# Weighing hyperedge blocks from PSUM in a fixed VectorE order, and spacing out the inverse degrees

## The chip, the cores and the metric

The kernel runs on one core of one Trainium2 chip. A core has TensorE (PE in the profile; PEld is its weight load), VectorE (DVE), ScalarE (ACT), GpSimd (POOL) and SyncE (SP, which only issues transfers here). Each works through its own list of instructions in order; a framework places the semaphores between them. SBUF is the working memory, PSUM the small memory that TensorE writes its products into, HBM the main memory. The metric is the device time of one execution in microseconds, the median of several.

## What is computed

Four graph layers on x (8 batches, 2048 nodes, 64 features) share one adjacency matrix. The change touches the first, whose core is cut from the reference here:

```python
h = x @ W
alpha = softmax(where(H.T > 0, leaky_relu(h @ a_node), NEG))         # nodes of a hyperedge
agg = einsum('ben,bnf->bef', alpha, h)                                # hyperedge features
beta = sigmoid((h @ a_gn)[:, None, :] + (agg @ a_ge)[:, :, None])
all_he = elu(beta[..., None] * h[:, None] + (1 - beta[..., None]) * agg[:, :, None])
coefs1 = softmax(where(H > 0, attn_scores(elu(agg))[:, None, :], NEG))
g = einsum('bne,benf->bnf', coefs1, all_he)                           # what the change computes
deg = maximum(adj.sum(-1), 1.0)[:, None]
industry = einsum('nm,bmf->bnf', adj / deg, x @ W_ind)                # uses the inverse degrees
```

The next layer uses 1 / sqrt(1 + row sum of the adjacency), which is taken from the same degrees.

## The kernel before

Most (node, hyperedge) pairs are empty. The kernel sorts the nodes by how many hyperedges they belong to and cuts them into 16 tiles of 128 nodes, one node a partition. Tile t has as many slots as its richest node needs: 12 for tile 0, then 5, 5, 4, 4, 4, four times 3, five times 2, and 1; 57 in all. One slot of one tile is a **block**: 128 nodes times 512 values (8 batches of 64 features). A loop over tiles and slots runs through the blocks:

- Three matmuls build z in a PSUM tile `pz`: the node's own row in two pieces (`hrh`, `hrl`, a high and a low part) through an identity, and the hyperedge's row through a one-hot matrix `o`.
- VectorE scales z in place by the ratio `R` (L793). ScalarE takes y = exp(z - 1) (L795). VectorE forms the elu from both, y = min(max(z, 1), y), into SBUF (L797); it is one above the elu, which is taken off later.
- VectorE weighs it with the softmax coefficient `co`: in the tile's first block into the sum `acc` (L800), otherwise in place in y (L802), and GpSimd adds y to acc (L803). After a tile's last block GpSimd scatters acc to HBM, `gs_hbm` (L805).

The PSUM tag "mm" has three buffers. They hold pz, and in between the transposed slot numbers of a coming tile (`slots`, once a tile), the transposed degrees `pdc` and four rows of inverse degrees `pinv`. A pz is free again when its last reader, L797, is done. The tag "y" has three SBUF buffers, acc two.

`begin(t)`, called in the first block of the tile ahead, fetches rows by an indirect transfer on GpSimd (L275), splits a row into its two pieces (ScalarE L167, GpSimd L168), issues small matmuls into `ps` and has VectorE compute R and co (L761, L764, L765, L767).

Between the blocks' matmuls the loop puts **filler**: `fill(n)` takes n steps of a generator, `products`, each step one 128x512 matmul of x times the adjacency, for use later in the layer. A block has five filler steps, and three more in the first block of a tile. `products` computes pair 0's first half, then the degrees of both halves of the columns (`degrees`, 64 matmuls with ones, its result evacuated in turns by ScalarE and VectorE at L110), then pair 0's second half and the other pairs. In pair 0's second half, from the third row tile on, every filler matmul also advances the generator `inverses` by one pass. It transposes the degrees, adds one (L366), lets GpSimd raise that to the power -0.5 (L367, `dinv`), overwrites the same SBUF tile with the degree of at least 1 (L368) and its reciprocal (L369), waits 20 passes, and then every four passes spreads a quarter of the reciprocals over a row, which ScalarE copies out (L378) and SP stores in `inv_hbm` (L379). The tile of these copies has two buffers.

TensorE's instructions are pinned to the order in which the program issues them (`keep_in_program_order`), as are GpSimd's row fetches and adjacency loads (two of the latter a block while there are any). The other engines' order in this loop is chosen by the framework's scheduler when the program is built. After the loop comes a stage that mixes the results; its TensorE list starts with 24 and 28 more filler steps before it needs what the scatters wrote.

Of the kernel before, what the change touches and what calls it, by code (L numbers as in the profile page):

```python
# [30 lines left out]
F32 = mybir.dt.float32  # L31
# [5 lines left out]
AF = mybir.ActivationFunctionType  # L37
ALU = mybir.AluOpType
AX = mybir.AxisListType
# [17 lines left out]
def tile_gnn_fast(  # L57
# [24 lines left out]
    nc = tc.nc  # L82
# [3 lines left out]
    P = 128  # L86
# [255 lines left out]
    def products():  # L342

        deg1 = hy.tile([P, NT], F32, name="deg1")

        def degrees(g):
            du = pph.tile([P, 2, C], F32, tag="ph", name=f"du{g}", bufs=2)
            for t in range(NT):
                for i in range(2):
                    mm(  # L350
                        du[:, i, :], lhsT=ones_r, rhs=adj_c(t, 2 * g + i), start=t == 0, stop=t == NT - 1
                    )
                    yield
            for i in range(2):
                c = 2 * g + i
                r = slice(c * P // NCH, (c + 1) * P // NCH)
                evacuate(deg4[r, :], du[r, i, :])

        def inverses():

            pdc = places["small"]([P, JT, P], "pdc")
            for j in range(JT):
                transpose(pdc[:, j, :], deg4[:, cols(j, P)])
            pdc = pdc.rearrange("p j (c r) -> p c j r", c=NCH)[:, :, :, 0]
            d1 = deg1.rearrange("p (c j) -> p c j", c=NCH)
            nc.vector.tensor_scalar(d1, pdc, 1.0, None, op0=ALU.add)  # L366
            nc.gpsimd.tensor_tensor(dinv, deg1, neg_half[:, :NT], ALU.pow)  # L367
            nc.vector.tensor_scalar(d1, pdc, 1.0, None, op0=ALU.max)  # L368
            nc.vector.reciprocal(deg1, deg1)  # L369
            for _ in range(20):  # L370
                yield
            for c in range(NCH):
                pt = places["small"]([P, C], "pinv")
                for j in range(JT):
                    k = c * JT + j
                    transpose(pt[:, cols(j, P)], deg1[:, k:k + 1].to_broadcast([P, P]))
                row = va.tile([P, C], F32, tag="ut", name="inv", bufs=2)
                nc.scalar.copy(row, pt)  # L378
                nc.sync.dma_start(inv_hbm[:, cols(c)], row)  # L379
                for _ in range(4):  # L380
                    yield

        for p in range(NP):
            for g in range(2):
                own = (2 * g, 2 * g + 1)
                ug = pph.tile([P, 2, C], F32, tag="ph", name="ug", bufs=2)
                u = {c: ug[:, c % 2, :] for c in own}
                turning = inverses() if p == 0 and g == 1 else iter(())
                for t in range(NT):
                    for i in range(2):  # L390
                        for c in own:
                            mm(
                                u[c], lhsT=part[t // JT][i][:, t % JT, :], rhs=adj_c(t, c),
                                start=t == 0 and i == 0, stop=t == NT - 1 and i == 1,
                            )
# [346 lines left out]
    with ExitStack() as pb_scope:  # L742
        pps = pb_scope.enter_context(tc.tile_pool(name="pb_ps", bufs=1, space=PSUM))
        places["small"] = lambda shape, name: pps.tile(shape, F32, tag="mm", name=name, bufs=3)
        pl = pb_scope.enter_context(tc.tile_pool(name="pl", bufs=1))

        def begin(t):
# [12 lines left out]
            R = pl.tile([P, 13, B], F32, tag="R", name="R", bufs=2)  # L760
            nc.vector.tensor_tensor(  # L761
                R[:, 0:S], ps[:, 0:S, 0, :], hrow[:, None, BF:BF + 8].to_broadcast([P, S, B]), ALU.add
            )
            nc.vector.tensor_reduce(R[:, S], ps[:, 0:S, 1, :].rearrange("p s b -> p b s"), AX.X, ALU.add)  # L764
            nc.vector.reciprocal(R[:, 0:S + 1], R[:, 0:S + 1])  # L765
            co = pl.tile([P, 12, B], F32, tag="co", name="co", bufs=2)
            nc.vector.tensor_tensor(  # L767
                co[:, 0:S], ps[:, 0:S, 1, :], R[:, S:S + 1, :].to_broadcast([P, S, B]), ALU.mult
            )
            return S, both, ohs, R, co  # L770


        tiles = [*range(NT - 2), NT - 1, NT - 2]
        now = begin(0)
        slots(tiles[1], pps, "mm", 3)
        for k, t in enumerate(tiles):
            S, both, ohs, R, co = now
            acc = pl.tile([P, B, F], F32, tag="acc", name="acc", bufs=2)
            for s in range(S):
                pz = pps.tile([P, C], F32, tag="mm", name="pz", bufs=3)  # L780
                for i, (l, r) in enumerate(((ident_r, both[0]), (ident_r, both[1]), (ohs[s], tab2))):
                    mm(pz, lhsT=l, rhs=r, start=i == 0, stop=i == 2)
                if s == 0 and k + 1 < NT:
                    fill(3)
                    now = begin(tiles[k + 1])
                fill(5)
                for _ in range(2):
                    if to_load:
                        load_adj(*to_load.pop(0))
# [3 lines left out]
                nc.vector.tensor_tensor(z, z, R[:, s, :, None].to_broadcast([P, B, F]), ALU.mult)  # L793
                y = pl.tile([P, B, F], F32, tag="y", name="y", bufs=3)
                nc.scalar.activation(y, z, AF.Exp, bias=-1.0)  # L795

                nc.vector.scalar_tensor_tensor(y, z, 1.0, y, op0=ALU.max, op1=ALU.min)  # L797
                cb = co[:, s, :, None].to_broadcast([P, B, F])
                if s == 0:
                    nc.vector.tensor_tensor(acc, y, cb, ALU.mult)  # L800
                else:
                    nc.vector.tensor_tensor(y, y, cb, ALU.mult)  # L802
                    nc.gpsimd.tensor_tensor(acc, acc, y, ALU.add)  # L803

            nc.gpsimd.indirect_dma_start(  # L805
                out=gs_hbm[:], out_offset=bass.IndirectOffsetOnAxis(ap=order[:, t:t + 1], axis=0),
                in_=acc.rearrange("p b f -> p (b f)"), in_offset=None,
            )

    hrp_scope.close()  # L810
    hy_scope.close()
# [1793 lines left out]
```

## Time and profile before

| what | us |
|---|---|
| median of three runs (1749.34 to 1750.75) | 1750.03 |
| the profiled execution's own time | 1747.23 |
| its span | 1745.0 |
| TensorE busy over the span | 1662.8 (95%) |
| VectorE, ScalarE, GpSimd busy | 832.9, 588.9, 573.6 |
| first and last matmul of the blocks (pz) start | 67.0 and 223.7 |
| last scatter issued | 231.7 |

The block loop takes about 165 us of the 1745. Lines of the profile name the engine, the source line, the operation and its tiles (out<-in); "x57" is the count, then come busy time and the mean of one in ns, then the engine's idle time just before them and what ended it. L172 is the helper through which most matmuls go, L175 that of the transposes, so these are told apart by tile names. Tile names are shortened by the profile (`co1` and `co2` are one name). Matmul durations overlap: a 128x512 matmul shows 0.39 to 0.40 us, but a filled queue starts one every 0.23.

### The profile page before, as it was taken

The page shows a single profiled execution, that of the slowest core. Times are in us where ns is not written, and L with a number is a line of the kernel's source. Part 1 is how long each engine was busy: PE and PEld are TensorE (multiplying, and loading weights), DVE is VectorE, ACT ScalarE, POOL GpSimd, SP SyncE. Part 2 cuts the span into 40 slices and gives each one's busy share as a digit, 9 for nine tenths or more (in the row PEclk, how much of TensorE's full clock was granted, in tenths as well). Part 3 has the DMA queues.
Part 4 walks back from the last instruction along what each step waited for, and adds up shares of the span by engine and source line. Part 5 has one row for each costly group of instructions (what it writes and reads, how often), then busy time and mean ns, then how long its engine had stood idle before and what let it go on. Part 6 is the DMA issues. An engine that isn't in the chain of part 4 may idle for free. (4 is left out here: it accounts for less than half of the span.)

```text
span 1745.0 us, 27987 instructions
## 1 busy us (share of the span) xinstructions
PE 1662.8 (95%) x11196; PEld 1214.8 (70%) x11196; DVE 832.9 (48%) x1547; ACT 588.9 (34%) x1031; POOL 573.6 (33%) x515
## 2 busy tenths in 40 slices
PE   6888899999989999999999989999989999999996
PEld 4666666666664444468788878888768877878775
DVE  7679945678642221210137147777623433433332
ACT  1345533434321212112213257878512222222221
POOL 4578845556534443422023001222310200202001
PEclk9899999999999999999999989999989999999998
DMA  9743344444340000017344547585571121211111
GB/s 334 253 158 124 103 131 140 151 140 145 97 141 6 30 19 12 24 66 292 111 140 130 137 105 157 133 171 131 150 273 43 49 61 43 61 47 42 57 43 39
DMA packets 171180, 195.83 MB, mean 112 GB/s; under 512 B 71536, under 2 KB 116336, under 8 KB 169760
## 3 DMA queue, kind: packets, MB, share of 16 engines
q1 hardware_dynamic: 160096, 154.54, 30.0%
q0 software_dynamic: 8544, 30.68, 5.3%
q10 hardware_dynamic: 2400, 8.72, 1.4%
q8 instruction: 90, 1.47, 0.4%
q14 instruction: 50, 0.41, 0.1%
HBM read 126.72 MB, written 67.17 MB: 111 GB/s over the span
## 5 line engine op out<-in xcount | busy, mean ns | idle before, releaser
L172 PE MATMUL ua<-pt,xn 128*128 128x512 f32 x512 | 230.2, 592 | 1.4 <-DVE pt L1150 1.4
L172 PEld LDWEIGHTS ua<-pt,xn 128*128 128x128 f32 x512 | 96.9, 190 | 111.1 <-issue 104.0
L1502 DVE COPY w_half<-pw 128x512 f32<-128x512 f32 x160 | 109.7, 705 | 91.2 <-PE pw L172 90.6
L1498 ACT COPY w_half<-pw 128x1024 f32<-128x1024 f32 x128 | 129.8, 1014 | 51.4 <-PE pw L172 51.4
L172 PE MATMUL py<-w_half,xg 128*32 128x128 f32 x4096 | 142.6, 280 | 1.2 <-issue 1.2
L172 PE MATMUL u<-adj,v0h 128*128 128x512 f32 x384 | 134.0, 426 | 1.1 <-ACT h L1800 1.1
L172 PE MATMUL u<-adj_more,v2h 128*128 128x512 f32 x384 | 126.5, 408 | 0.0
L172 PEld LDWEIGHTS py<-w_half,xg 128*32 128x32 f32 x4096 | 111.6, 138 | 18.9 <-issue 2.1
L172 PE MATMUL u<-adj,v0l 128*128 128x512 f32 x384 | 124.6, 402 | 0.0
L172 PE MATMUL u<-adj_more,v2l 128*128 128x512 f32 x384 | 124.2, 400 | 0.0
L172 PE MATMUL pw<-est,wst 64*128 64x256 f32 x1024 | 111.2, 322 | 4.9 <-ACT w_half L1498 2.7
L1156 POOL TENSOR_TENSOR acc<-acc,pt 128x512 f32<-128x512 f32 x60 | 76.5, 1274 | 104.3 <-DVE pt L1150 103.6
L172 PEld LDWEIGHTS pw<-est,wst 64*128 64x128 f32 x1024 | 84.5, 189 | 27.6 <-ACT w_half L1498 20.0
L1150 DVE TENSOR_SCALAR pt<-pt 128x512 f32<-128x512 f32 x64 | 29.6, 462 | 153.0 <-ACT pt L1149 152.8
L1709 ACT CAST ar<-fcav 128x512 fp32r<-128x512 f32 x64 | 39.5, 618 | 166.8 <-DMA fcav<-in_adj_t 165.9
L172 PE MATMUL u<-adj_more,v3l 128*128 128x512 f32 x288 | 94.2, 403 | 0.0
L172 PE MATMUL u<-adj,v1h 128*128 128x512 f32 x288 | 93.7, 403 | 0.0
L1149 ACT ACTIVATE pt<-s 128x512 f32<-128x512 f32 x64 | 38.0, 598 | 164.8 <-PE s L172 164.8
L172 PE MATMUL u<-adj_more,v3h 128*128 128x512 f32 x288 | 93.6, 403 | 0.0
L1710 DVE SCALAR_TENSOR_TENSOR ar<-fcav,ar 128x512 f32<-128x512 f32 x64 | 44.7, 698 | 100.9 <-ACT ar L1709 100.9
L172 PE MATMUL u<-adj,v1l 128*128 128x512 f32 x288 | 92.0, 397 | 0.0
L1681 POOL TENSOR_TENSOR x<-x,rows 128x512 f32<-128x512 f32 x16 | 22.7, 1439 | 210.8 <-PE pt L175 129.3
(406 smaller groups left out, 3282.6 us busy)
## 6 DMA issues: line engine op xcount, KB each, us to landing
fcav<-in_adj_t SPq DMA_DIRECT2D x64, 256.0 KB, 2.9
u_hbm<-ut SPq DMA_DIRECT2D x48, 256.0 KB, 2.8
xg<-u_hbm SPq DMA_DIRECT2D x24, 512.0 KB, 8.5
adj<-in_adj_t POOLq DMA_DIRECT2D x16, 512.0 KB, 7.7
adj_more<-in_adj_t POOLq DMA_DIRECT2D x16, 512.0 KB, 7.7
adj_hbm<-adj_more SPq DMA_DIRECT2D x16, 512.0 KB, 5.5
x_hbm<-r SPq DMA_DIRECT2D x28, 256.0 KB, 2.7
hs_hbm<-st ACTq DMA_DIRECT2D x8, 584.0 KB
```

Of the source, the lines that this page charges most:

```text
L172: tc.keep_in_program_order(nc.tensor.matmul(*args, **kw))
L1149: nc.scalar.activation(pt, s, AF.Exp)
L1150: nc.vector.tensor_scalar(pt, pt, 1.0, None, op0=ALU.max)
L1156: nc.gpsimd.tensor_tensor(accs[c], accs[c], pt, ALU.add)
L1498: pin(nc.scalar.copy(dst, pw.rearrange("p j o n -> p n (j o)")))
L1502: pin(copy(dst[:, :, 2 * j:2 * j + 2], bank.rearrange("p o n -> p n o")))
L1681: nc.gpsimd.tensor_tensor(xs, xs, b2.to_broadcast([P, JT, P]), ALU.add)
L1709: nc.scalar.copy(ar, seen_a)
L1710: nc.vector.scalar_tensor_tensor(ar.bitcast(F32), seen_a, 1.0, ar.bitcast(F32), op0=ALU.mult, op1=ALU.not_equal, accum_out=left[:, t, k:k ...
```

## The change

The elu is written back into PSUM, over z, and weighed from there; in a block that isn't a tile's first the product goes to a new SBUF tile y, which shares the tag "y" and its three buffers with the exp's result. The weighing of a block is put off: it is held in a list `rest` and issued in the next block, between that block's exp and its elu. With it go the GpSimd add and, behind a tile's last block, the scatter. R and co of the next tile are computed by `ratios()`, which is issued after the elu of the tile's first block and no longer in `begin`. All VectorE instructions of the loop are held in program order. In `inverses`, the degree of at least 1 and its reciprocal come 16 passes after the power has been issued, the first row 4 passes later, and the rows 11 passes apart. The degrees' evacuations are given to ScalarE and VectorE by name, VectorE's held in order.

```diff
@@ degrees
-                evacuate(deg4[r, :], du[r, i, :])
+                if i:
+                    tc.keep_in_program_order(nc.vector.tensor_copy(deg4[r, :], du[r, i, :]))
+                else:
+                    nc.scalar.copy(deg4[r, :], du[r, i, :])
@@ inverses
-            nc.vector.tensor_scalar(d1, pdc, 1.0, None, op0=ALU.add)
+            kept = tc.keep_in_program_order
+            kept(nc.vector.tensor_scalar(d1, pdc, 1.0, None, op0=ALU.add))
             nc.gpsimd.tensor_tensor(dinv, deg1, neg_half[:, :NT], ALU.pow)
-            nc.vector.tensor_scalar(d1, pdc, 1.0, None, op0=ALU.max)
-            nc.vector.reciprocal(deg1, deg1)
-            for _ in range(20):
+            for _ in range(16):
+                yield
+            kept(nc.vector.tensor_scalar(d1, pdc, 1.0, None, op0=ALU.max))
+            kept(nc.vector.reciprocal(deg1, deg1))
+            for _ in range(4):
                 yield
...
-                for _ in range(4):
+                for _ in range(11):
                     yield
@@ begin: the four VectorE instructions move into a function, each held
+            def ratios():
+                hold(nc.vector.tensor_tensor(
+                    R[:, 0:S], ps[:, 0:S, 0, :], hrow[:, None, BF:BF + 8].to_broadcast([P, S, B]), ALU.add
+                ))
...
+            return S, both, ohs, R, co, ratios
@@ the loop
         now = begin(0)
+        now[-1]()
         slots(tiles[1], pps, "mm", 3)
+        rest = []
+
+        def weighed(acc, z, cb, first, t):
+            if first:
+                hold(nc.vector.tensor_tensor(acc, z, cb, ALU.mult))
+            else:
+                y = pl.tile([P, B, F], F32, tag="y", name="y", bufs=3)
+                hold(nc.vector.tensor_tensor(y, z, cb, ALU.mult))
+                nc.gpsimd.tensor_tensor(acc, acc, y, ALU.add)
+            if t is not None:
+                nc.gpsimd.indirect_dma_start(
+                    out=gs_hbm[:], out_offset=bass.IndirectOffsetOnAxis(ap=order[:, t:t + 1], axis=0),
+                    in_=acc.rearrange("p b f -> p (b f)"), in_offset=None,
+                )
...
-                nc.vector.tensor_tensor(z, z, R[:, s, :, None].to_broadcast([P, B, F]), ALU.mult)
-                y = pl.tile([P, B, F], F32, tag="y", name="y", bufs=3)
-                nc.scalar.activation(y, z, AF.Exp, bias=-1.0)
-
-                nc.vector.scalar_tensor_tensor(y, z, 1.0, y, op0=ALU.max, op1=ALU.min)
+                hold(nc.vector.tensor_tensor(z, z, R[:, s, :, None].to_broadcast([P, B, F]), ALU.mult))
+                e = pl.tile([P, B, F], F32, tag="y", name="e", bufs=3)
+                nc.scalar.activation(e, z, AF.Exp, bias=-1.0)
+                if rest:
+                    rest.pop()()
+
+                hold(nc.vector.scalar_tensor_tensor(z, z, 1.0, e, op0=ALU.max, op1=ALU.min))
+                if s == 0 and k + 1 < NT:
+                    now[-1]()
                 cb = co[:, s, :, None].to_broadcast([P, B, F])
-                if s == 0:
-                    nc.vector.tensor_tensor(acc, y, cb, ALU.mult)
-                else:
-                    nc.vector.tensor_tensor(y, y, cb, ALU.mult)
-                    nc.gpsimd.tensor_tensor(acc, acc, y, ALU.add)
-
-            nc.gpsimd.indirect_dma_start(
-                out=gs_hbm[:], out_offset=bass.IndirectOffsetOnAxis(ap=order[:, t:t + 1], axis=0),
-                in_=acc.rearrange("p b f -> p (b f)"), in_offset=None,
-            )
+                rest.append(lambda z=z, acc=acc, cb=cb, s=s, t=t, S=S: weighed(
+                    acc, z, cb, s == 0, t if s == S - 1 else None
+                ))
+        rest.pop()()
```

More of the change, by code (lines that the diff above doesn't have):

```diff
@@ L745, in tile_gnn_fast @@
         pl = pb_scope.enter_context(tc.tile_pool(name="pl", bufs=1))
+        hold = tc.keep_in_program_order
         def begin(t):
@@ L760, in begin @@
             R = pl.tile([P, 13, B], F32, tag="R", name="R", bufs=2)
-            nc.vector.tensor_tensor(
-                R[:, 0:S], ps[:, 0:S, 0, :], hrow[:, None, BF:BF + 8].to_broadcast([P, S, B]), ALU.add
-            )
-            nc.vector.tensor_reduce(R[:, S], ps[:, 0:S, 1, :].rearrange("p s b -> p b s"), AX.X, ALU.add)
-            nc.vector.reciprocal(R[:, 0:S + 1], R[:, 0:S + 1])
-            co = pl.tile([P, 12, B], F32, tag="co", name="co", bufs=2)
[L767 to L770, printed above, removed]
+            co = pl.tile([P, 12, B], F32, tag="co", name="co", bufs=2)
+            def ratios():
+                hold(nc.vector.tensor_tensor(
+                    R[:, 0:S], ps[:, 0:S, 0, :], hrow[:, None, BF:BF + 8].to_broadcast([P, S, B]), ALU.add
+                ))
+                hold(nc.vector.tensor_reduce(
+                    R[:, S], ps[:, 0:S, 1, :].rearrange("p s b -> p b s"), AX.X, ALU.add
+                ))
+                hold(nc.vector.reciprocal(R[:, 0:S + 1], R[:, 0:S + 1]))
+                hold(nc.vector.tensor_tensor(
+                    co[:, 0:S], ps[:, 0:S, 1, :], R[:, S:S + 1, :].to_broadcast([P, S, B]), ALU.mult
+                ))
+            return S, both, ohs, R, co, ratios
         tiles = [*range(NT - 2), NT - 1, NT - 2]
         now = begin(0)
+        now[-1]()
         slots(tiles[1], pps, "mm", 3)
+        rest = []
[11 more added lines that the diff above has]
+                )
         for k, t in enumerate(tiles):
-            S, both, ohs, R, co = now
+            S, both, ohs, R, co, _ = now
             acc = pl.tile([P, B, F], F32, tag="acc", name="acc", bufs=2)
@@ L792, in tile_gnn_fast @@
                 z = pz.rearrange("p (b f) -> p b f", f=F)
-                nc.vector.tensor_tensor(z, z, R[:, s, :, None].to_broadcast([P, B, F]), ALU.mult)
-                y = pl.tile([P, B, F], F32, tag="y", name="y", bufs=3)
-                nc.scalar.activation(y, z, AF.Exp, bias=-1.0)
-                nc.vector.scalar_tensor_tensor(y, z, 1.0, y, op0=ALU.max, op1=ALU.min)
-                cb = co[:, s, :, None].to_broadcast([P, B, F])
-                if s == 0:
-                    nc.vector.tensor_tensor(acc, y, cb, ALU.mult)
-                else:
-                    nc.vector.tensor_tensor(y, y, cb, ALU.mult)
-                    nc.gpsimd.tensor_tensor(acc, acc, y, ALU.add)
-            nc.gpsimd.indirect_dma_start(
-                out=gs_hbm[:], out_offset=bass.IndirectOffsetOnAxis(ap=order[:, t:t + 1], axis=0),
-                in_=acc.rearrange("p b f -> p (b f)"), in_offset=None,
-            )
+                hold(nc.vector.tensor_tensor(z, z, R[:, s, :, None].to_broadcast([P, B, F]), ALU.mult))
[6 more added lines that the diff above has]
+                    now[-1]()
+                cb = co[:, s, :, None].to_broadcast([P, B, F])
+                rest.append(lambda z=z, acc=acc, cb=cb, s=s, t=t, S=S: weighed(
+                    acc, z, cb, s == 0, t if s == S - 1 else None
+                ))
+        rest.pop()()
     hrp_scope.close()
```

## The prediction

> **What bounds the kernel now.** I read the page's slices first, then busy time by stretch for the stage that the diff touches, then its groups with shapes kept apart, then the waits, then the timeline of single engines. The page's chain of waits reaches back only to 1286 us, so it says nothing of this stage; the stretches must. The scatters of the 16 tiles (108.4, 119.4, 136.7, 146.7, 160.4, 169.3, 176.4, 184.3, 193.0, 202.6 ... 224.3, 227.8, 231.7) give the time of each tile. Busy time by stretch, 68 to 238 us:
> ```profile
> core 0: us, PE busy (x) PEld busy (x) DVE busy (x) ACT busy (x) POOL busy (x), PEclk, DMA share, GB/s
> 68.00:102.00 34.00, 30.22 (x114) 22.59 (x113) 24.77 (x39) 13.13 (x37) 23.73 (x28) 0.88 1.08 368
> 102.00:120.00 18.00, 16.22 (x72) 12.57 (x72) 17.48 (x31) 10.19 (x29) 14.06 (x11) 1.00 0.16 55
> 120.00:156.00 36.00, 28.20 (x133) 21.44 (x131) 27.86 (x49) 17.86 (x42) 29.33 (x22) 1.00 0.36 113
> 156.00:190.00 34.00, 32.19 (x145) 25.61 (x146) 33.51 (x60) 21.39 (x60) 29.39 (x23) 1.00 0.31 106
> 190.00:224.20 34.20, 29.15 (x117) 21.02 (x116) 29.39 (x57) 17.86 (x44) 29.98 (x25) 0.95 0.35 111
> 224.20:238.30 14.10, 14.08 (x59) 10.69 (x57) 4.14 (x8) 2.89 (x5) 4.93 (x5) 1.00 0.16 60
> ```
> TensorE runs one in-order list of matmuls, blocks and filler alike, and after the last block it is full (14.08 of 14.10). Up to 500 us it stays near full, so what the change can win is TensorE's idle time in these blocks: 3.8, 1.8, 7.8, 1.8 and 5.1 us, 20.2 in all. VectorE is behind it in the second and fourth stretch, GpSimd close to it in the last. The groups of the blocks (67 to 232 us):
> ```profile
> L803 POOL TENSOR_TENSOR acc<-acc,y 128x512 f32<-128x512 f32 x41 | 56.9, 1388 | 14.5 <-DVE y L802 11.9 <-DVE R L764 1.3 <-PE pz L172 0.4
> L802 DVE TENSOR_TENSOR y<-y,co 128x512 f32<-128x512 f32 x41 | 40.4, 1002 | 0.2
> L793 DVE TENSOR_TENSOR pz<-pz,R 128x512 f32<-128x512 f32 x57 | 38.3, 686 | 9.6 <-PE pz L172 7.2 <-ACT o L300 1.3 <-issue 1.0
> L797 DVE SCALAR_TENSOR_TENSOR y<-pz,y 128x512 f32<-128x512 f32 x57 | 37.8, 677 | 7.2 <-ACT y L795 6.6
> L800 DVE TENSOR_TENSOR acc<-y,co 128x512 f32<-128x512 f32 x16 | 17.4, 1086 | 0.9 <-DMA gs_hbm<-acc,order 0.9
> ```
> The two weighings (L802, L800) are the only ones of these that read both inputs from SBUF, and the only ones far above 0.69 us. Spread of three operations (min/median/max):
> ```profile
> L802 DVE TENSOR_TENSOR y<-y,co x41: 674/691/3445, 78.1 to 227.7; 128x512 f32<-128x512 f32 x41
> L800 DVE TENSOR_TENSOR acc<-y,co x16: 675/866/2372, 71.7 to 227.1; 128x512 f32<-128x512 f32 x16
> L885 DVE TENSOR_TENSOR ind<-pi,inv x16: 673/690/693, 240.1 to 442.3; 128x512 f32<-128x512 f32 x16
> ```
> L885 is the new weighing's shape exactly (PSUM and SBUF in, SBUF out) and never goes over 0.693. VectorE's timeline at the inverse degrees:
> ```profile
> 125.43 0.69 DVE L797 SCALAR_TENSOR_TENSOR y<-pz,y 128x512 f32<-128x512 f32 x1
> 130.84 0.17 DVE L368 TENSOR_SCALAR deg<-pdc 128x16 f32<-128x16 f32 x1 [4.72 <-POOL dinv L367]
> 130.93 0.68 DVE L802 TENSOR_TENSOR y<-y,co 128x512 f32<-128x512 f32 x1
> ```
> L368 overwrites what GpSimd's power still reads, and all of VectorE's blocks stand behind it. TensorE's and VectorE's own waits:
> ```profile
> PE pz L172 <- DVE y L797: 10.3, 13, 1.7
> PEld pz L172 <- issue: 10.5, 9, 2.0
> DVE pz L793 <- PE pz L172: 7.2, 10, 1.6
> DVE y L797 <- ACT y L795: 6.6, 7, 2.4
> ```
> The first is the third PSUM buffer coming free at L797.
>
> [...] L802 reaches 3.445 us, L793 with one SBUF input never passes 0.700. [...] the trace shows no such difference (0.690 against 0.691), so I charge none.
>
> **The change part by part.**
>
> *Weighing from PSUM.* 57 weighings at 0.69 are 39.3 us instead of 40.4 + 17.4 = 57.8: 18.5 us of VectorE gone. GpSimd's adds go from 1.388 to about 1.29 (their median): 41 x 0.1 = 4 us. L797 now writes PSUM; L793, which does so, takes 0.686 against 0.677: +0.5 us[...]. The exp's tile and the weighed tile are now two allocations of the same three buffers, so exp of block s+3 still waits for the add of block s, as before: nothing, provided that GpSimd isn't later.
>
> *Order and lateness.* VectorE's order is scale(s), weigh(s-1), elu(s). In a filled queue such operations start 0.60 apart. The elu waits for scale 0.69 + exp 0.60 + about 0.09 of handover (75.09 to 76.45 in the timeline is 1.36), while the weighing fills 0.6 of that: a block is 1.36 + 0.60 = 1.96, rounded to 1.98, if ScalarE is free. Queued behind a late exp now stand the elu, the next scale and the next weighing; GpSimd and the PSUM buffers wait for those. ScalarE is 50% busy, 48 us of it in 164 with other pieces of 0.3 to 0.6: 0.29 x 0.3 = 0.1 us on average, up to 0.6 where one full piece is ahead each time; I take 0.2, so 2.18 a block. Ratios of the next tile (R and co) cost 0.55 to 0.75 a tile as before, now after elu(0), where the tile still has a block or more to go: nothing, or 0.7 late in tiles of one or two blocks.
>
> *PSUM held longer.* A block's buffer comes free at weigh(s), inside block s+1, instead of at the elu: some 1.3 us later. The third buffer covers this except where the slot transpose takes it, once a tile: then the next three matmuls (0.95 from the waiting one to the scale, at 95.30 to 96.27) stand against one elu of 0.6, so 0.25 to 0.35 for 15 tiles, 3.5 to 5 us; nothing where GpSimd is the later one.
>
> *Adds and scatters.* The last weighing of a tile, its add and its scatter move into the next tile's block 0, behind that tile's row fetch and split on GpSimd's queue if the order follows the program (1.3 + 1.3 us). The following scatters wait for one another anyway (4.5 us of such waits); the gathered rows are read after 237 us, and 52 filler matmuls cover 13 us there. At nothing; up to 2 us if the last scatter is later by that.
>
> *Inverse degrees.* L368 and L369 come 16 passes later, some three blocks, 6 us or more; the power takes 2.95 behind at most two adds (2.6). The 4.72 us stall goes; what is late next is the third PSUM buffer, which the transposed degrees now hold for those three blocks: 3 x 0.5 = 1.5 us back. The four rows come 11 passes apart, over 4 us, against a store that lands in 3.8: ScalarE's wait of 3.84 us on it at 143 goes too. On SP, inverse row loads (first at 144.1) move to about 160, past u and x transfers that are used only after 230: nothing. Two evacuations per half keep their engines; only the order of VectorE's is fixed: nothing.
>
> *Sum, tile by tile against the scatters.* Tile 0 (12 blocks): the repeated 0.30 us wait of TensorE for L797 and 0.39 of VectorE for TensorE at 93 to 101 go, since a scale no longer runs three blocks ahead: 2.5 of the 3.8 idle. Tiles of 5: 2 x (5 x 2.18 + 0.75) = 23.3 for 28.3: -5. Tiles of 4: VectorE 4 x 2.18 + 0.7 = 9.4, GpSimd 3 adds, row fetch, split and scatter of 1.3 each and 4 parts in three tiles, 9.5; 28.5 + 1.5 = 30 for 32.6: -2.6. Tiles of 3: TensorE 31 instructions x 0.234 = 7.26 against VectorE's 7.2: no more than the idle 1.8. Tiles of 2: GpSimd 4 x 1.3 = 5.2 for 5.4 now: -0.5. Together -12.4; less 3.5 for the slot buffer, about -9. The profiled execution took 1747.23 (span 1745.0 and 2.2 around), so 1738.2; its runs have the median 1750.03, 2.8 above it, so **1741 us**.
>
> **Rivals.** *GpSimd paces it:* its pieces add up to 41 x 1.29 + 43 x 1.3 to 1.35 + 9 + 3 + 10.8 = 132 of 164 us; if its order, not its speed, makes the idle time, only part of the 4.7 stall is won: -2, 1748. For it: tiles of 2 at 5.4. Against it: 11.9 us in which adds wait for L802. *Nearly all idle time goes:* -16, 1734, if the slot buffer costs nothing. *ScalarE's exp paces a rigid VectorE:* the 156 us up to the last block are 57 blocks and 15 tiles' ratios of 10 us, so 2.56 us a block now. With 1.98 + d a block, d over 0.58 makes it slower; at d = 0.7, 57 x 0.12 = +7: 1757. For it: today's order lets other blocks pass a late exp, and ScalarE waits 10.9 us for slot transposes with exps behind it. Against it: exp follows scale within 0.1 us wherever ScalarE is idle.
>
> **How the numbers follow.** Forecast 0.60 (own range 1733 to 1746), GpSimd 0.15, nearly all 0.08, rigid order 0.17. A measurement tells about 0.2%, 3.5 us, from no change: faster 0.68, same 0.15, slower 0.17. The range 1732 to 1755 leaves out most of the largest gain and the upper part of the rigid order, under 0.2, and takes in the slot buffer at nothing and at 5 us and the late scatter.
>
> **What would show it.** Weighings at 0.69 at most 0.70; adds at 1.29; no wait of L368's successor on the power above 1 us; the last block's matmuls near 215 instead of 224; TensorE's wait for PSUM now on the weighing. Wrong if VectorE's elu waits for exp more than 0.58 a block, or if TensorE's idle time up to the last block stays at 20 us.

## The result, and the profile after

The changed kernel takes 1747.16 us (median of 22 runs, 1739.81 to 1752.07) against 1749.82 for the kernel before beside it (22 runs). The ratio is 0.9982, 95% interval 0.9971 to 0.9992: 3.2 us gained where 9 were forecast. Its profiled execution has a span of 1743.1 us.

Busy time by stretch, the same stretches as shown of before; the columns are engine busy time (with instruction counts), granted TensorE clock, DMA share and GB/s:

```profile
core 0: us, PE busy (x) PEld busy (x) DVE busy (x) ACT busy (x) POOL busy (x), PEclk, DMA share, GB/s
68.00:102.00 34.00, 31.12 (x134) 23.71 (x132) 25.18 (x44) 16.24 (x44) 28.03 (x32) 1.00 1.06 375
102.00:120.00 18.00, 13.54 (x57) 9.75 (x56) 14.62 (x27) 7.26 (x18) 8.36 (x7) 1.00 0.14 46
120.00:156.00 36.00, 30.71 (x142) 23.10 (x142) 28.38 (x56) 21.22 (x52) 30.42 (x24) 1.00 0.40 122
156.00:190.00 34.00, 30.01 (x132) 22.84 (x131) 26.56 (x54) 19.13 (x49) 25.86 (x22) 1.00 0.29 97
190.00:224.20 34.20, 31.73 (x140) 24.50 (x139) 26.80 (x58) 17.51 (x43) 26.85 (x24) 1.00 0.33 110
224.20:238.30 14.10, 11.58 (x45) 7.78 (x45) 2.13 (x8) 2.29 (x4) 2.51 (x3) 0.90 0.52 160
```

The last block's matmuls start at 217.1 us instead of 223.3. TensorE's idle time up to 217 has hardly changed, though: 2.9, 4.5, 5.3, 4.0 us in the first four stretches, where before had 3.8, 1.8, 7.8, 1.8. It fell where the inverse degrees are computed (120 to 156), and rose in front of that and behind it. From the first block's matmuls to the last block's it is 19.1 us, and was 20.2. Most of the rest of the difference is TensorE's clock in these two executions: over the matmuls of tile 0 (67.0 to 100.2 us before, 65.5 to 94.1 here) it was 0.86 of full speed before and 0.95 here, and the 108 matmuls recorded there in each kept TensorE busy for 29.4 us before and 26.3 here.

The last stretch now has gaps (11.58 of 14.10), where TensorE waits for the scattered rows to be read back. This wait isn't new: before had it behind 238.3 us, outside the stretch, and it is as long. TensorE's waits between the last block and 310 us, before and after (total us, times, longest):

```profile
PE pg L175 <- DMA gn<-gs_hbm: 2.4, 2, 1.7
PE pg L175 <- DMA gn<-gs_hbm: 2.5, 1, 2.5
```

Groups of the blocks (67 to 232 us), with count, busy time and mean in ns, then the idle time ahead and what ended it:

```profile
L798 POOL TENSOR_TENSOR acc<-acc,y 128x512 f32<-128x512 f32 x41 | 53.0, 1293 | 21.1 <-DVE y L797 20.3 <-PE pz L172 0.3 <-PE ps L172 0.2
L828 DVE SCALAR_TENSOR_TENSOR pz<-pz,e 128x512 f32<-128x512 f32 x57 | 39.8, 698 | 21.7 <-ACT e L824 19.0
...
L797 DVE TENSOR_TENSOR y<-pz,co 128x512 f32<-128x512 f32 x41 | 28.1, 686 | 7.2 <-POOL acc L798 6.6
L794 DVE TENSOR_TENSOR acc<-pz,co 128x512 f32<-128x512 f32 x16 | 10.9, 681 | 0.3 <-DMA gs_hbm<-acc,order 0.3
```

The weighings (L797, L794) are at 0.686 and 0.681 us; the long ones of before are gone. The adds (L798) are at 1.293. All of that is as predicted. But the elu (L828) now has 21.7 us of idle time in front of it. The waits of VectorE and of TensorE in the loop say for what (total us, times, longest):

```profile
DVE pz L828 <- ACT e L824: 19.0, 18, 2.2
DVE y L797 <- POOL acc L798: 6.6, 11, 1.7
DVE pz L822 <- PE pz L172: 2.4, 5, 0.9
...
PE pz L172 <- ACT slot L288: 7.8, 12, 1.0
PE pz L172 <- DVE acc L794: 4.5, 5, 1.5
PE pz L172 <- DVE y L797: 4.3, 5, 1.4
```

VectorE waits for exp 18 times, 19.0 us in all, where it was 6.6 us in 7 before. TensorE's wait for a PSUM buffer is now for ScalarE's copy of the slot numbers (7.8) and for the weighings (4.5 and 4.3), where it was for the elu (10.3) and these two:

```profile
PE pz L172 <- ACT slot L288: 2.8, 4, 1.0
PE pz L172 <- DVE R L764: 2.6, 2, 1.7
```

The three largest waits of TensorE add up to 16.6 us after and 15.7 before: they have changed their names, and TensorE stands as long.

Where the waits of 2 us lie can be seen at the start of tile 1. ScalarE's timeline (start, duration):

```profile
95.31 0.60 ACT L824 ACTIVATE e<-pz 128x512 f32<-128x512 f32 x1 [1.42 <-DVE pz L822]
97.56 0.53 ACT L288 CAST slot<-pslot 64x128 bf16<-64x128 f32 x2 [1.65 <-PE pslot L175]
98.11 0.69 ACT L299 ACTIVATE far<-slot,number 128x128 bf16<-128x128 bf16 x2
98.72 0.49 ACT L300 ACTIVATE o<-far 128x128 fp32r<-128x128 bf16 x2
99.11 0.68 ACT L299 ACTIVATE far<-slot,number 128x128 bf16<-128x128 bf16 x2
99.70 0.49 ACT L300 ACTIVATE o<-far 128x128 fp32r<-128x128 bf16 x2
100.10 0.57 ACT L824 ACTIVATE e<-pz 128x512 f32<-128x512 f32 x1
```

and VectorE's in the same microseconds:

```profile
96.91 0.69 DVE L822 TENSOR_TENSOR pz<-pz,R 128x512 f32<-128x512 f32 x1
97.79 0.69 DVE L797 TENSOR_TENSOR y<-pz,co 128x512 f32<-128x512 f32 x1 [0.19 <-POOL acc L798]
100.70 0.70 DVE L828 SCALAR_TENSOR_TENSOR pz<-pz,e 128x512 f32<-128x512 f32 x1 [2.23 <-ACT e L824]
```

The block's scale begins at 96.91 and takes 0.69, so exp could run from 97.7. ScalarE is then at the slot numbers of tile 3: two copies, and for each of that tile's four slots two activations (L299, L300). Exp starts at 100.10, and the elu, at the head of VectorE's queue, waits 2.23 us. In the loop, `slots` stands ahead of the exp; the old VectorE order took other blocks' work meanwhile, the fixed one can't. In the two tiles of 5 VectorE waits 4.3 us for exp in this way, where before it waited there for none. Of the 19.0 us, 16.7 fall in eleven such blocks, two in tile 0 and one in a later tile; the tiles of 4 show hardly any.

The time from one tile's first block matmul to the next tile's, read from TensorE's timeline of each kernel's profile and added up by number of slots (us). "Loop" runs from the first block's matmuls to the last block's, "idle" is TensorE's idle time in it:

| kernel | tile 0 (12 slots) | 2 tiles of 5 | 3 of 4 | 4 of 3 | 5 of 2 | loop | idle | total, ratio to before |
|---|---|---|---|---|---|---|---|---|
| before | 33.2 | 26.1 | 35.7 | 29.5 | 31.8 | 156.3 | 20.2 | 1 |
| the change | 28.5 | 31.6 | 31.9 | 32.3 | 27.2 | 151.6 | 19.1 | 0.9982 |
| e1 inverses only | 32.2 | 27.5 | 35.7 | 29.6 | 31.8 | 156.7 | 19.3 | 1.0004 |
| e2 PSUM weighing only | 37.4 | 28.8 | 36.2 | 31.2 | 26.7 | 160.2 | 24.2 | 1.0014 |
| e3 order left free | 38.4 | 27.0 | 31.6 | 29.3 | 26.6 | 152.8 | 18.8 | 0.9988 |
| e4 one-hots after exp | 29.8 | 28.4 | 31.9 | 30.5 | 27.1 | 147.7 | 14.9 | 0.9936 |
| e5 fixed in tile 0 only | 29.0 | 28.1 | 33.2 | 29.3 | 26.6 | 146.2 | 12.9 | 0.9940 |
| e6 e5 with e4 | 29.3 | 28.1 | 32.3 | 29.1 | 26.6 | 145.4 | 12.2 | 0.9924 |
| e7 e4, slot before filler | 28.1 | 27.9 | 33.9 | 28.8 | 26.9 | 145.6 | 13.0 | 0.9925 |
| e8 e4, exp its own buffer | 30.1 | 27.6 | 30.3 | 29.9 | 27.1 | 145.0 | 12.2 | 0.9917 |
| e9 weighed from SBUF | 31.7 | 30.5 | 33.9 | 30.7 | 31.6 | 158.3 | 20.5 | 1.0001 |
| e10 inverses undone | 30.0 | 35.4 | 35.0 | 33.3 | 27.3 | 161.0 | 24.1 | 1.0028 |
| e11 all three edits | 29.4 | 26.2 | 30.1 | 27.7 | 26.9 | 140.3 | 9.1 | 0.9883 |
| e12 e6, slot before filler | 29.2 | 25.9 | 31.4 | 27.8 | 26.9 | 141.2 | 11.7 | 0.9906 |

One profile is one execution, with its own luck of the clock (tile 0 ran at 0.85 to 0.96 of full speed in these profiles), so the ratios carry the verdicts and the table says where.

### The profile page after: what moved, and what is told of

Same layout as the page of the kernel before. It is cut to its first block, busy times and chain, and to the rows that moved or that the text cites. A ratio compares the mean times of both kernels' runs of the same rounds, so it can differ in the third digit from the quotient of the medians.

```text
span 1743.1 us, 27974 instructions
## 1 busy us (share of the span) xinstructions
PE 1660.5 (95%) x11196; PEld 1210.7 (69%) x11196; DVE 818.2 (47%) x1547; ACT 589.8 (34%) x1031; POOL 562.2 (32%) x515
## 3 DMA queue, kind: packets, MB, share of 16 engines
q1 hardware_dynamic: 160096, 154.54, 30.5%
## 4 chain that ended last, share of the span: by engine, by line
PE 85%; DMA 5%; DVE 3%; ACT 2%; issue 2%; POOL 1%; SPq 1%; POOLq 0%; ACTq 0%; DVEq 0%
PE u L172 38%; PE ua L172 13%; PE py L172 8%; PE ug L172 6%; PE pw L172 6%; PE pr L172 2%; PE pz L172 2%; PE pf L172 2%; PE po L172 1%; PE pt L175 1%; PE s L172 1%; PE pd L172 1%; DMA est<-est_hbm 1%; PE pi L172 1%; PE ph L606 1%
## 5 line engine op out<-in xcount | busy, mean ns | idle before, releaser
L172 PEld LDWEIGHTS pw<-est,wst 64*128 64x128 f32 x1024 | 84.3, 189 | 28.3 <-ACT w_half L1525 18.7
L1177 DVE TENSOR_SCALAR pt<-pt 128x512 f32<-128x512 f32 x64 | 29.7, 463 | 152.8 <-ACT pt L1176 152.6
```

The source lines that it names most:

```text
L172: tc.keep_in_program_order(nc.tensor.matmul(*args, **kw))
L1177: nc.vector.tensor_scalar(pt, pt, 1.0, None, op0=ALU.max)
```

## Experiments

Four kernels ran beside the kernel before in each of three rounds of experiments; ratios are to it, with a 95% interval in brackets.

**e1: the inverse degrees alone.** The kernel before with this part of the change, and the degrees' evacuations by name:

```diff
...
+            kept(nc.vector.tensor_scalar(d1, pdc, 1.0, None, op0=ALU.add))
             nc.gpsimd.tensor_tensor(dinv, deg1, neg_half[:, :NT], ALU.pow)
-            nc.vector.tensor_scalar(d1, pdc, 1.0, None, op0=ALU.max)
...
+            for _ in range(16):
+                yield
+            kept(nc.vector.tensor_scalar(d1, pdc, 1.0, None, op0=ALU.max))
...
-                for _ in range(4):
+                for _ in range(11):
```

> The kernel before with the inverse degrees' spacing (and the degrees' evacuations by name) alone. Theory A (the change's gain is the inverse degrees' stall; the blocks themselves win nothing because VectorE's fixed order gives back what the PSUM weighing frees): VectorE's 4.7 us wait for the power and ScalarE's 3.8 us wait for the row store go, tiles 2 and 3 (14.1 and 13.7 us between first matmuls) become 2 to 4 us shorter together, total 2 to 4 us less than before, so as good as the whole change (-3.2). Theory B (the gain is the PSUM weighing): at most 1 us less than before, since GpSimd paces tile 2 anyway. Tile 0 of this kernel is as before: if its 33.2 us were the throttled clock's (0.69 in 70 to 80 us), it may come out near 29 here too, as in the changed kernel.

Measured: 1.0004 (0.9994 to 1.0014). VectorE's 4.7 us wait for the power is gone from its list of waits, and the total doesn't move. Tiles 2 and 3 take 15.4 and 15.0 us instead of 14.1 and 13.7; tile 4 takes 10.5 instead of 11.6. Theory A misses: in the old kernel the stall's removal alone is worth nothing. Theory B's number holds, but not its reason, as e2 shows.

**e2: weighing from PSUM alone.** The scheduler's order, the old inverse degrees, no putting off (e is the exp's tile; the weighed y is a tile of its own):

```diff
-                nc.vector.scalar_tensor_tensor(y, z, 1.0, y, op0=ALU.max, op1=ALU.min)
+                nc.vector.scalar_tensor_tensor(z, z, 1.0, e, op0=ALU.max, op1=ALU.min)
...
-                    nc.vector.tensor_tensor(y, y, cb, ALU.mult)
+                    nc.vector.tensor_tensor(y, z, cb, ALU.mult)
```

> The kernel before with the elu written back to PSUM and weighed from there at once, in the order that the scheduler chooses; inverse degrees as before. Theory A: VectorE's weighings fall to 0.69 us (18 us less busy), GpSimd's adds to 1.29, but the total moves by less than 2 us, because TensorE waits for PSUM buffers and GpSimd as before. Theory B: 4 to 8 us less than before, mostly in the tiles of 3 to 5 slots. [...]

Measured: 1.0014 (1.0005 to 1.0024), 2.5 us slower. The weighings fall to 0.686, so VectorE is freed as wanted; its wait for block matmuls grows from 7.2 us to 19.9, since TensorE now gets its PSUM buffer back only after the weighing:

```profile
DVE pz L793 <- PE pz L172: 19.9, 22, 3.6
PE pz L172 <- DVE y L803: 10.5, 10, 1.5
```

The freed 18 us of VectorE are not the bound: the longer hold of PSUM costs at least as much as they give. By the table the loss lies in tile 0, where TensorE idles 8.3 us instead of 3.8; the tiles of 2 become 5 us shorter, up to 1.7 of it by the clock of the execution before (an estimate: two of these tiles, 8.7 and 5.9 us long, ran at 0.85 and 0.93 there).

**e3: the changed kernel, order left free.**

```diff
-        hold = tc.keep_in_program_order
+        hold = lambda i: i
```

> The changed kernel with VectorE's order in the blocks left to the scheduler. If the fixed order is what gives the gain back (an elu at the head of the queue waiting 19.0 us in all for late exps), VectorE's wait for exp falls under 8 us and the total is 4 us or more below the changed kernel's (so 7 below before). If the fixed order is a gain (no scale running three blocks ahead), the total is 2 to 5 us above the changed kernel's, about that of before.

Measured: 0.9988 (0.9978 to 0.9997), not told apart from the changed kernel. VectorE's wait for exp falls to 4.7 us, as the first theory had it, but neither total came. Under that lie two large effects: tile 0 takes 10 us more (TensorE idles 9.6 us there instead of 2.3) and the other tiles 8.6 us less (114.5 against 123.1). VectorE's timeline in tile 0 of this kernel:

```profile
95.01 0.70 DVE L822 TENSOR_TENSOR pz<-pz,R 128x512 f32<-128x512 f32 x1 [0.27 <-PE pz L172]
95.62 0.68 DVE L797 TENSOR_TENSOR y<-pz,co 128x512 f32<-128x512 f32 x1
97.42 0.70 DVE L822 TENSOR_TENSOR pz<-pz,R 128x512 f32<-128x512 f32 x1 [1.12 <-PE pz L172]
```

The next scale waits 1.12 us for its matmuls after the weighing that frees their buffer, a block every 2.41 us. The changed kernel, also in tile 0:

```profile
75.84 0.69 DVE L822 TENSOR_TENSOR pz<-pz,R 128x512 f32<-128x512 f32 x1
76.44 0.68 DVE L797 TENSOR_TENSOR y<-pz,co 128x512 f32<-128x512 f32 x1
77.26 0.70 DVE L828 SCALAR_TENSOR_TENSOR pz<-pz,e 128x512 f32<-128x512 f32 x1
77.86 0.69 DVE L822 TENSOR_TENSOR pz<-pz,R 128x512 f32<-128x512 f32 x1
```

Here scale follows scale after 2.02 us (1.98 was worked out), without a gap.

**e4: one-hots after the exp.** The changed kernel; the one-hot activations of a coming tile are collected and issued one a block behind the exp (in the tile's last block all that are left):

```diff
-                    slots(tiles[k + 2], pps, "mm", 3)
+                    slots(tiles[k + 2], pps, "mm", 3, ones_to_do)
...
                 nc.scalar.activation(e, z, AF.Exp, bias=-1.0)
+                if ones_to_do:
+                    ones_to_do.pop(0)()
```

> The changed kernel with ScalarE's one-hot matrices of a coming tile (two activations each) issued one a block after the block's exp, where the changed kernel issues all of a tile's before the exp of one block. Theory A2 (the step that failed is the lateness of exp: not 0.2 us spread over all blocks but 2.2 us once a tile, when four or five one-hots stand before the exp): VectorE's wait for exp falls from 19 to 5 to 9 us, tiles of 5 slots from 14.6 and 17.0 to 12 and 14 us, the total 5 to 10 us below the changed kernel's. Rival (the slot copy's PSUM buffer or GpSimd sets the pace): the wait for exp falls, another wait grows by as much, the total within 2 us of the changed kernel's.

Measured: 0.9936 (0.9917 to 0.9954), against 0.9982 (0.9971 to 0.9992) for the changed kernel; the difference is 8 us. ScalarE at the start of tile 1:

```profile
97.25 0.53 ACT L296 CAST slot<-pslot 64x128 bf16<-64x128 f32 x2 [1.65 <-PE pslot L175]
97.81 0.40 ACT L286 ACTIVATE far<-slot,number 128x128 bf16<-128x128 bf16 x1
98.12 0.58 ACT L836 ACTIVATE e<-pz 128x512 f32<-128x512 f32 x1
```

Exp comes after one activation, not eight: it starts at 98.12, and the elu's wait there is 0.52 us. VectorE's waits:

```profile
DVE pz L844 <- ACT e L836: 13.9, 20, 1.4
DVE y L809 <- POOL acc L810: 5.4, 8, 1.7
```

19.0 us became 13.9. In the tiles of 5 the wait for exp falls from 4.3 us to 1.1 and the time by 3.2, which fits; they take 13.1 and 15.3 us where 12 and 14 were expected, and the tiles of 3 lose 1.8. The wait fell by less than expected and the total by as much as expected, so the rival is out. Of the 8 us, the profiles show 3.9 in the loop, though tile 0 had the lower clock here (0.89 against 0.95), and 1.5 behind it, where the wait for the scattered rows falls from 2.5 us to 1.0; the rest isn't located.

**e5 and e6: order fixed in tile 0 only**, without and with the late one-hots.

```diff
-        hold = tc.keep_in_program_order
+        fixed = [True]
+        hold = lambda i: tc.keep_in_program_order(i) if fixed[0] else i
...
             S, both, ohs, R, co, _ = now
+            fixed[0] = k == 0
```

> The changed kernel with VectorE's order held in tile 0 alone and left to the scheduler in the other 15. If the fixed order is a gain in tile 0 (28.5 us between first matmuls there, 38.4 with the free order) and a loss behind it (123.1 for tiles 1 to 15 against 114.4), the two add up: tile 0 at 28 to 30, the other tiles at 114 to 117, the total 5 to 9 us below the changed kernel's, so 8 to 12 below before. If the free order's 114.4 only paid off what tile 0 had left behind (GpSimd or the scatters late), the other tiles come out at 121 or more and the total within 2 us of the changed kernel's.

> Order held in tile 0 alone and the one-hots issued one a block after the exp. If one-hots ahead of an exp hurt only where VectorE can't pass the waiting elu, this equals the better of the two edits alone: tiles 1 to 15 at 113 to 117 us, total within 3 us of the kernel with the late one-hots (1734.7). If they hurt in any order, it is 3 to 6 us below both.

Measured: 0.9940 (0.9927 to 0.9953) and 0.9924 (0.9912 to 0.9936). The gain of the fixed order in tile 0 can be had without its price behind it: 29.0 and 117.2 us in e5. The tiles behind come out some 3 us above e3's, at the edge of what was expected. With VectorE free behind tile 0, the late one-hots add nothing that these runs tell apart (the intervals overlap), where they gave 8 us with the fixed order. So it is the fixed order that made their place matter, as far as these runs tell: the two gains added would be 15 us, and e6 has 10.

**e7: slot numbers before the filler.** e4 with the call of `slots` moved from behind `fill(5)` to ahead of it.

> The kernel with late one-hots and fixed order, with the slot transpose (and ScalarE's two copies of it) put ahead of the block's five filler matmuls. The slot copy then falls into the time of the scale. Theory (the third PSUM buffer is lost to the slot numbers, some 0.6 us a tile for TensorE and as much for the exp behind the copies): TensorE's wait for the slot copy (7.2 us in 11) nearly goes, VectorE's wait for the exp falls from 13.9 to 6 to 9, total 3 to 6 us below the kernel with late one-hots. Rival (GpSimd paces the tiles of two and three slots): the waits move, the total within 2 us.

Measured: 0.9925 (0.9912 to 0.9937). TensorE's waits for the slot copy (7.2 us) are gone from the list and VectorE's wait for exp falls to 9.3, while its wait for GpSimd's adds rises from 5.4 us to 7.6; the loop is 2.0 us shorter. The totals of e4 and e7 can't be told apart, so theory and rival stay open.

**e8: one buffer for exp.** e4 with

```diff
-                e = pl.tile([P, B, F], F32, tag="y", name="e", bufs=3)
+                e = pl.tile([P, B, F], F32, tag="e", name="e", bufs=1)
...
-                y = pl.tile([P, B, F], F32, tag="y", name="y", bufs=3)
+                y = pl.tile([P, B, F], F32, tag="y", name="y", bufs=2)
```

> The kernel with late one-hots and fixed order; of the three buffers that exp's result and the weighed tile share, one is given to exp alone and two to the weighed tile. In the fixed order an exp never starts before the elu of the block before is done, so one buffer is enough. If the shared buffers cost nothing, as predicted, VectorE's wait for GpSimd's add stays at 5.4 us and the total within 2 us of the kernel with late one-hots; if exps hold the buffers that the weighed tiles need, that wait falls under 2 us and the total by 2 to 4.

Measured: 0.9917 (0.9904 to 0.9930). The wait of the weighing for GpSimd's add (5.4 us) is gone, so the shared buffers did cost something, and the loop is 2.7 us shorter, most of it in the tiles of 4. The totals again overlap.

**e9: weighed from SBUF, all else as changed.**

```diff
-                hold(nc.vector.scalar_tensor_tensor(z, z, 1.0, e, op0=ALU.max, op1=ALU.min))
+                hold(nc.vector.scalar_tensor_tensor(e, z, 1.0, e, op0=ALU.max, op1=ALU.min))
...
-                hold(nc.vector.tensor_tensor(y, z, cb, ALU.mult))
-                nc.gpsimd.tensor_tensor(acc, acc, y, ALU.add)
+                hold(nc.vector.tensor_tensor(z, z, cb, ALU.mult))
+                nc.gpsimd.tensor_tensor(acc, acc, z, ALU.add)
```

(z is e in these two lines, passed in by the loop.)

> The changed kernel (fixed order, weighing put off by a block, inverse degrees spaced) with the elu written to SBUF and weighed there in place, as before the change. PSUM is free again at the elu. If the PSUM weighing is worth something inside the fixed order (18 us less of VectorE, 4 us less of GpSimd), this is 4 to 8 us above the changed kernel's, 1 to 5 above before; weighings back at 0.9 to 1.0 us on average. [...]

Measured: 1.0001 (0.9990 to 1.0012), 3.3 us above the changed kernel (the two intervals just overlap), a little less than expected. The weighings of this kernel (min/median/max ns):

```profile
L796 DVE TENSOR_TENSOR e<-e,co x41: 674/798/3957, 80.9 to 234.3; 128x512 f32<-128x512 f32 x41
...
L794 DVE TENSOR_TENSOR acc<-e,co x16: 680/682/3093, 78.4 to 233.0; 128x512 f32<-128x512 f32 x16
```

Up to 3.957 us for the same product that takes at most 0.694 from PSUM. In the fixed order the PSUM weighing is worth about 3 us, net of the longer hold of PSUM; alone (e2) it cost 2.5. Its gain lies in the tiles of 2: 31.6 us here, 27.2 in the changed kernel; the granted clock was 1.00 in both from 190 to 217 us. VectorE is busy for 30.1 us there when it weighs from SBUF, and for 21.5 when it weighs from PSUM. GpSimd's adds take 1.297 us here, so in the fixed order they are short with either source; in the free order they were short only with PSUM (1.287 in e2, 1.388 before).

**e10: inverse degrees as before, all else as changed.** The reverse of e1's diff.

> The changed kernel with the inverse degrees as before (both VectorE instructions right behind the power, rows four passes apart). Alone in the old kernel the spacing gave nothing (1.0004). If the stall counts in the fixed order, where nothing passes it, this is 2 to 5 us above the changed kernel's, with the 3 to 5 us wait for the power back; if the PSUM buffer held by the transposed degrees costs what the stall gives, it is within 1.5 us.

Measured: 1.0028 (1.0016 to 1.0040), 8 us above the changed kernel, more than either theory gave. VectorE's timeline, the wait for the power and one of the late exps behind it:

```profile
130.93 0.18 DVE L368 TENSOR_SCALAR deg<-pdc 128x16 f32<-128x16 f32 x1 [3.73 <-POOL dinv L367]
...
137.40 0.70 DVE L822 SCALAR_TENSOR_TENSOR pz<-pz,e 128x512 f32<-128x512 f32 x1 [2.49 <-ACT e L818]
```

Beside these 3.7 us, VectorE's wait for exp is 27.0 us instead of 19.0, and TensorE waits 3.8 us for the transposed degrees' PSUM buffer and 2.4 for row copies.

**e11 and e12: the edits together.** e11 is e4 with e7's and e8's; e12 is e6 with e7's.

> Fixed order, late one-hots, slot before the filler, exp with one buffer of its own. The waits that the three edits remove are different ones (one-hots 5 us, slot copy 7 us of TensorE, add 5 us), so if TensorE is what all of them hold up, the total is 2 to 4 us below the best so far (0.9917 of before): 0.989 to 0.991. If GpSimd's 130 us of work now sets the pace, it stays at 0.991 to 0.993.

> Order held in tile 0 alone, late one-hots, slot before the filler. With VectorE free to pass a late exp the slot copies should matter less than with the fixed order: 0 to 2 us below the kernel with tile 0 fixed and late one-hots (0.9924 of before).

Measured: 0.9883 (0.9864 to 0.9903) and 0.9906 (0.9890 to 0.9923). e11 takes 1728.98 us beside 1748.03 for before: the fastest median here, about 17 us below the changed kernel by the ratios, and a little better than expected. e12 gains 3 us on e6 where at most 2 were expected, with intervals that overlap; those of e11 and e12 overlap too. The stretches and waits of e11:

```profile
102.00:120.00 18.00, 16.18 (x69) 11.93 (x69) 16.86 (x32) 9.16 (x24) 11.22 (x11) 1.00 0.26 89
120.00:156.00 36.00, 33.31 (x159) 25.86 (x158) 30.57 (x60) 22.53 (x55) 33.42 (x27) 1.00 0.41 135
156.00:190.00 34.00, 33.24 (x150) 26.35 (x149) 29.96 (x63) 22.74 (x62) 29.41 (x26) 1.00 0.34 106
```

```profile
DVE pz L844 <- ACT e L836: 12.2, 22, 1.4
DVE y L809 <- POOL acc L810: 1.6, 4, 0.5
...
PE pz L172 <- DVE y L809: 3.2, 4, 1.1
```

TensorE idles 1.8, 2.7 and 0.8 us there, where the changed kernel had 4.5, 5.3 and 4.0.

## Why the prediction was wrong

The direction was right, and the size three times too large. Of the two signs of being wrong that the prediction named, one came true: TensorE's idle time up to the last block stayed at 20 us (20.2 before, 19.1 after). The other did not: VectorE waits 0.33 us a block for exp, not over 0.58. By its steps:

- **"I take 0.2, so 2.18 a block": the step that failed.** Exp's lateness was spread over all blocks as an average of ScalarE's other pieces. It measures 19.0 us in 57 blocks, 0.33 a block, and even that mean is not the point: it comes in lumps, in the one block of a tile whose exp stands behind the coming one-hots and the copies in front of them, 2.23 us with four one-hots. Tiles of 5 were put at 23.3 us and took 31.6. e4 moves only these activations and wins 8 us; e5 lets VectorE pass them and wins 7; e6 does both and wins 10. So this cause is shown: the fixed order turned the one-hots' place in ScalarE's queue into a wait of VectorE's. The rival of a rigid order named this mechanism. Its turning point of 0.58 a block is passed only in tiles 7, 10 and 12 (0.65 to 0.81), and the tiles of 5 lost time at 0.45, so a mean per block told nothing there either.
- **The rest of the tiles of 5.** The one-hots are 3.2 us of the 8.3 by which these tiles missed. e11 gets them to 26.2 us, and TensorE is busy for 23.1 of these: the 23.3 left it next to no idle time. The prediction also took its times of before between scatters (28.3 us for the tiles of 5, 32.6 for those of 4), where the first matmuls give 26.1 and 35.7. For both groups together it forecast -7.6 us; the change has +1.7, and e11 -5.5.
- **Weighing from PSUM: right in its prices.** 0.69 was forecast and 0.686 and 0.681 measured; adds 1.29 and 1.293, but e9 has 1.297 from SBUF, so the fixed order alone would have shortened them. The elu into PSUM takes 0.698 instead of 0.677, 1.2 us in all where 0.5 was charged. By e9 these 18 us of VectorE are worth some 3 us of time.
- **Tiles of 2: where the PSUM weighing pays.** -0.5 was forecast, with GpSimd as their bound, and -4.5 measured, of which, by the estimate at e2, up to 1.7 is the clock. Every kernel that weighs from PSUM takes 26.6 to 27.3 us here, and the three that weigh from SBUF 31.6 to 31.8. So it is partly luck that the direction came out right: the tiles of 5 and 3 lost 8.4 us, and a term that was put at almost nothing helped to make up for them.
- **Slot numbers' buffer: right in place and near in size.** 3.5 to 5 us were charged; TensorE waits 7.8 us in 12 for it, 5.0 more than before, and e7, which removes this wait on top of e4, shortens the loop by 2.0.
- **Shared buffers at nothing: wrong.** VectorE waits 6.6 us for adds, and e8 removes that wait; the loop gains 2.7 us.
- **Inverse degrees: right only within the fixed order.** Alone they give nothing (e1), where the sum had 4.7 less 1.5. In the fixed order they are worth 8 us (e10). The prediction had added a stall's length to a sum; in the old order TensorE's idle time fell by only 0.9 us without the stall.
- **Tile 0: right, once the clock is taken out.** 2.5 us were forecast and 4.7 measured at unlike clocks. At the same clock of 0.89, e10 takes 30.0 us where e1, in the old order, takes 32.2; at 0.86, e8 takes 30.1 where before takes 33.2. Against the free order with PSUM weighing (e3) it is 10 us: without a fixed order, the longer hold of PSUM would have made tile 0 slower.
- **Tiles of 4 and of 3.** -3.9 us against -2.6 for those of 4, measured between other marks; those of 3 lost 2.9 where -1.8 was forecast, and e4 gives 1.8 of that back.
- **Adds and scatters at nothing: right.** TensorE waits 2.5 us for the scattered rows, 2.4 before.
- **GpSimd as the bound, the second rival:** not at 1748. e11 does the same GpSimd work in a loop of 140.3 us.

What stays open: how the 8 us of e10 divide between the wait for the power, the PSUM buffers and the later exps they push; what took the stall's place in e1; and whether e7's and e8's edits each win time alone, since their totals overlap with e4's.

## What to carry to other kernels

When an engine's order is fixed, go through the queue of the engine that feeds it and add up what stands ahead of each input at the worst place, not on average: here eight short activations in front of one exp of a tile, in a queue that was half idle. An edit that frees an engine is worth nothing until the wait that takes its place is priced: the same edit cost 2.5 us in one order of work and won some 3 in another, and what it won lay where VectorE had been full. The length of a stall seen in a trace is not its worth either: taking away one of 4.7 us was worth nothing in the old order and, with the rows spaced out, 8 us in the new one.

## What the runs showed of the hardware

Weighings with both inputs in SBUF reach 3.445 us before (L802, median 0.691) and 3.957 us in e9 (L796, median 0.798), longer than one add (1.3) and a weighing (0.69) together. The timeline around the longest (e9) shows what lies beside it, GpSimd first and then VectorE:

```profile
213.35 1.30 POOL L168 TENSOR_TENSOR v2l<-xc,v2h 128x512 fp32r<-128x512 f32 x1
214.59 2.55 POOL L168 TENSOR_TENSOR hrl<-hrow,hrh 128x512 fp32r<-128x512 f32 x2
213.74 3.96 DVE L796 TENSOR_TENSOR e<-e,co 128x512 f32<-128x512 f32 x1
```

Three GpSimd instructions run without a gap until 217.14, and the weighing ends 0.56 us behind the last of them, as if it had stood until then. The one of 3.445 us in the execution before has two beside it, 171.57 to 174.12, and ends at 174.67. Of the 57 weighings of that execution 17 took over 1 us, and each of the 17 ends 0.54 to 0.57 us behind the end of a GpSimd add (L803) or split (L168) that ran beside it. That a weighing stands until GpSimd is done, and through more than one of its instructions where they follow each other closely, is read from these ends alone: the profile counts the whole time as the weighing's own. With one input in PSUM none of the changed kernel's 57 took over 0.694.

For reading from PSUM instead of SBUF the prediction charged nothing, and the medians show no difference: 0.690 us from PSUM (L885 of before, and L797 of the changed kernel), 0.691 from SBUF (L802 of before). The elu takes 0.698 and 0.694 us into PSUM (the change, e2) and 0.677 and 0.687 into SBUF (before, e9), about 0.01 to 0.02 us less.

Which part of the first 100 us ran at a lowered TensorE clock differed from one execution to the next: in 68 to 84 us it was 0.74 in the execution before and 0.99 in the changed one. Tile 0 of the kernel before takes 33.2 us at 0.86, and e1, which leaves tile 0 as it was, 32.2 at 0.89. So a comparison of two profiles tile by tile can be off by up to some 4 us in tile 0 (an estimate: 29.4 us busy at 0.86 would be 25.3 at full clock, and the 26.3 at 0.95 in the changed kernel would be 25.0).
